# Counting more of a graph's edges: 308 nodes instead of 200, int16 counts, one-hots by ScalarE

## The chip, the cores and the metric

The kernel runs on one core of a Trainium2 chip. Its engines work side by side, each through its own queue in order: TensorE (PE; its weight loads are shown as PEld), VectorE (DVE), ScalarE (ACT), GpSimd (POOL), and SyncE (SP), which here only starts transfers. Tiles lie in SBUF, 128 partitions wide; results of matmuls lie in PSUM, which has banks of 512 f32 per partition. The metric is the time of one execution on the device, in microseconds (us). The kernel before took 1614.48 us, the median of three runs (1614.27 to 1616.7).

## The reference

One layer on 6250 nodes of 256 features and 100,000 edges, all in f32. Cut to what matters:

```
xn = layernorm(x)
neigh = segment_sum(xn[src], dst)              # one row of 256 per edge, added to its target
g = batchnorm(relu(((1 + eps) * xn + neigh) @ W1 + b1) @ W2 + b2) * gamma + beta
m = mixer(xn)                                  # linear attention over all nodes, then gelu(. @ w1) @ w2
x = x + g + m
x = x + ffn(layernorm(x))                      # an LSTM along the nodes, hidden size 256, and a gate
```

The edges come sorted by target (`dst`), and the targets are denser at the low end: a target is 6250 times the square of an even draw. So the first edges share few targets, each of which receives many rows.

## The kernel before

**Preparation (0 to about 70 us).** The rows are loaded and normalised (`xn`), written back to memory as `xn_d`, and also kept transposed (`xnT`). The sources (`si`) and targets of the edges are brought into columns: 782 edge tiles of 128 edges, in `GROUPS` = 196 groups of four (`GT` = 4). Two checks on the targets are kept in `within` (lines 289 to 309): each group's targets must span fewer than `W` = 96 nodes, and in the counted part each pair of tiles must span fewer than `CW` = 8 nodes, all below `CN`. If a check fails, a slow fallback redoes the sums (lines 740 to 775).

**The edge loop (about 72 to 909 us).** It builds `sums`, the transposed neighbour sums, in two ways.

- *The gathered part*: groups 34 to 195. For each tile GpSimd gathers 128 rows of `xn_d` (L390) into one of ten buffers `eg`. VectorE builds a selection matrix `here` from the targets (L401). TensorE multiplies them (L411), and VectorE adds the result into a window of `sums` (L421), whose place is read from a register.
- *The counted part*: the first `COUNTED` = 34 groups, 136 tiles in 68 pairs. Nothing is gathered. `count_job` makes, for each edge, a one-hot of 128 for the low bits of its source (ScalarE: `Square` of a ramp less the value, then `Relu` of 1 less that, L621 and L622) and a one-hot of 392 for the source's block of 128 and the target within the window of eight nodes (VectorE `is_equal`, L623). Their product (L629, bf16) counts how often each source occurs for each target; VectorE adds it into a window of `counts` (L636), which holds for 49 blocks of 128 sources (`NB`) `CN` = 200 targets, f32. At the end `rows_job` loads the rows of `xn_d` three blocks at a time (L646), TensorE multiplies them with the counts (L654) into one PSUM bank for both halves of the features, and VectorE adds the result to `sums` (L659).

**Other jobs in the loop.** Around the groups the kernel runs jobs written as generators. `kv_job` (50) makes keys and values and their normalisation: a matmul (L441), a bias add on VectorE (L446), a `Square` on ScalarE (L449), a reduction (L454) and a `Sqrt` on ScalarE (L456), a chain of small VectorE operations from the reciprocal (L460) to L471, then the outer products (L475, L479). `gin_job` (50) applies W1 and W2 to 125 nodes whose sums are complete (L597, L603, L608, L613). `fold_job`, `own_job` and `mix_job` belong to the mixer.

**What sets the order.** Lines 688 to 703 give every job its first slot; a slot is one turn of the loop at line 709, with one group. In every slot each running job makes one step. The order on TensorE, VectorE and ScalarE is exactly the order of issue. In a slot that order is: the gathers of the group two ahead, the add of the last group, the selections of the next, the jobs' steps by age, then the four tiles' matmuls with the jobs' matmuls spread between them, and last the variance steps of kv jobs. Transfers of `rows_job` and `own_job` stand in SyncE's queue in the same order.

**After the loop (909 us to the end).** Statistics of the batch norm, then the LSTM stage, then the output. It starts once the last gin jobs are done.

## Time and profile before

| | |
|---|---|
| median of three runs | 1614.48 us (1614.27 to 1616.7) |
| profiled execution | 1617.26 us |
| its span in the profile | 1615.2 us |
| granted TensorE clock, mean | 0.966 |
| busy: TensorE, VectorE, ScalarE, GpSimd | 1483.9, 943.9, 612.0, 680.7 us |
| gathers | 646, from 71.8 to 887.9 us, 961 ns each |
| last gin matmuls done | about 909 us |

The profile is of one execution. Busy time is the union of an engine's instructions; matmuls overlap one another, so TensorE can be shown as busy and still take more. An idle time is put down to what ended it. In the row of digits below, each digit is the busy share, in tenths, of a slice of about 40 us.

### The profile page before, as it was taken

To read this page: it belongs to the slowest core of one execution; us is meant where nothing else is said; L and a number is where in the kernel's file an instruction comes from. 1 tells how busy PE (TensorE), PEld (TensorE's weight loads), DVE (VectorE), ACT (ScalarE), POOL (GpSimd) and SP (SyncE) were. 2 spreads that over 40 slices of the span, in tenths; PEclk is the share of its full clock that TensorE was granted. 3 is DMA by queue.
4 is the path that set the end of the run, shared out by engine and by line. 5 is a ranking of instruction groups with operands and counts; after the bars stand their busy time and mean duration, and the time that the engine had idled before them with its cause. 6 is when DMAs were issued, how large, how long until landed. Compare 5 with 4: busy or idle time off the path is not lost. (4 is left out here: it accounts for less than half of the span.)

```text
span 1615.2 us, 31225 instructions
## 1 busy us (share of the span) xinstructions
PE 1483.9 (92%) x11312; PEld 1388.5 (86%) x11312; DVE 943.9 (58%) x3027; ACT 612.0 (38%) x1867; POOL 680.7 (42%) x714
## 2 busy tenths in 40 slices
PE   1789898999989999999999599999999999999984
PEld 1488788989888999999989599999999998888864
DVE  6789888888742222222222385555555557777777
ACT  2833333343312222233222255445554434444440
POOL 2177777777777777777777000000000000000005
PEclk9799999999999999999999799999999999999996
DMA  9533333333444554444444021111111002233315
GB/s 245 194 105 105 105 104 104 105 102 106 133 137 141 151 156 144 122 119 123 120 123 142 29 90 64 65 65 52 65 65 65 14 1 77 90 92 92 94 45 160
DMA packets 64645, 166.03 MB, mean 103 GB/s; under 512 B 14347, under 2 KB 29436, under 8 KB 63228
## 3 DMA queue, kind: packets, MB, share of 16 engines
q0 software_dynamic: 31008, 84.71, 18.4%
q1 hardware_dynamic: 29822, 75.08, 14.3%
q10 hardware_dynamic: 3648, 4.10, 1.1%
q8 instruction: 93, 1.52, 0.4%
q14 instruction: 74, 0.61, 0.1%
HBM read 130.56 MB, written 33.28 MB: 101 GB/s over the span
## 5 line engine op out<-in xcount | busy, mean ns | idle before, releaser
L390 POOL DMA_INDIRECT eg<-xn_d,si x646 | 620.5, 961 | 257.8 <-issue 99.3
L411 PE MATMUL pg<-here,eg 128*128 128x96 f32 x2584 | 389.1, 276 | 32.5 <-DMA eg<-xn_d,si 30.3
L411 PEld LDWEIGHTS pg<-here,eg 128*128 128x128 f32 x2584 | 358.2, 195 | 63.2 <-DMA eg<-xn_d,si 34.4
L962 ACT ACTIVATE gate<-pg,b_l 128x125 f32<-128x125 f32 x718 | 201.9, 366 | 230.4 <-PE pg L953 229.1
L421 DVE TENSOR_TENSOR sums<-sums,pg 128x192 f32 x162 | 57.3, 353 | 349.3 <-PE pg L411 202.9
L920 PE MATMUL pg<-yT,w_ih 128*128 128x125 f32 x1600 | 188.4, 276 | 0.0
L920 PEld LDWEIGHTS pg<-yT,w_ih 128*128 128x128 f32 x1600 | 184.1, 193 | 0.0
L953 PE MATMUL pg<-sums,w_hh 128*128 128x125 f32 x1568 | 183.1, 275 | 0.0
L953 PEld LDWEIGHTS pg<-sums,w_hh 128*128 128x128 f32 x1568 | 179.0, 192 | 0.0
L889 POOL TENSOR_TENSOR ln_r<-ln_v,minus_half 125x1 f32<-125x1 f32 x50 | 27.4, 552 | 350.9 <-DVE ln_v L887 314.0
L1091 POOL TENSOR_TENSOR xr<-xr,rest_t 125x1024 f32<-125x1024 f32 x8 | 22.9, 2899 | 312.3 <-DVEq L1036 312.3
L953 PE MATMUL pg<-h_w,w_hh 128*128 128x125 f32 x1248 | 145.6, 275 | 0.0
L613 ACT ACTIVATE sums<-mm,vec 128x125 f32<-128x125 f32 x100 | 36.4, 365 | 281.4 <-DVE sums L421 232.8
L953 PEld LDWEIGHTS pg<-h_w,w_hh 128*128 128x128 f32 x1248 | 143.0, 192 | 0.0
L597 PE MATMUL mm<-sums,g 128*128 128x125 f32 x800 | 116.8, 282 | 2.6 <-DVE counts L636 2.5
L608 PE MATMUL mm<-z,g 128*128 128x125 f32 x800 | 115.5, 284 | 0.8 <-DVE stats L614 0.6
L597 PEld LDWEIGHTS mm<-sums,g 128*128 128x128 f32 x800 | 103.8, 195 | 6.0 <-issue 2.3
L441 PE MATMUL mm<-m,xr 128*125 128x256 f32 x400 | 107.8, 395 | 0.6 <-DVE counts L636 0.6
L608 PEld LDWEIGHTS mm<-z,g 128*128 128x128 f32 x800 | 102.6, 197 | 1.2 <-DVE stats L614 0.8
L449 ACT ACTIVATE mm<-kv 125x512 f32<-125x512 f32 x50 | 30.1, 602 | 186.4 <-DVE kv L446 186.4
L968 DVE TENSOR_TENSOR new<-gate,gate 128x125 f32<-128x125 f32 x178 | 51.5, 289 | 65.2 <-ACT gate L962 60.3
L401 DVE TENSOR_TENSOR here<-counts,drel 128x384 f32<-128x384 f32 x162 | 89.4, 552 | 0.0
(238 smaller groups left out, 2164.6 us busy)
## 6 DMA issues: line engine op xcount, KB each, us to landing
x_d<-x_out SPq DMA_DIRECT2D x40, 500.0 KB
x_in<-x_d SPq DMA_DIRECT2D x40, 500.0 KB
eg<-xn_d,si POOLq DMA_INDIRECT x646
counts<-xn_d SPq DMA_DIRECT2D x16, 384.0 KB
xn<-in_x_dram SPq DMA_DIRECT2D x5, 1120.0 KB
xn_d<-xn SPq DMA_DIRECT2D x5, 1120.0 KB
m<-in_x_dram SPq DMA_DIRECT2D x50, 112.0 KB
out_dram<-o SPq DMA_DIRECT2D x12, 448.0 KB
```

Source lines behind the costliest of these rows:

```text
L390: nc.gpsimd.indirect_dma_start(out=g, out_offset=None, in_=xn_d[:], in_offset=bass.IndirectOffsetOnAxis(ap=at, axis=0))
L401: nc.vector.tensor_tensor(here[:, :n, :], iota[:, None, :W].to_broadcast([P, n, W]), drel[:, gi * GT:gi * GT + n, None].to_broadcast([P, n ...
L411: nc.tensor.matmul(pg[:, k, :], g[:, k * P:(k + 1) * P], here[:, i, :], start=(i == 0 and k == 0), stop=(i == n - 1), skip_group_check=True)
L421: nc.vector.tensor_add(window, window, pg)
L441: nc.tensor.matmul(pkv[:r, at], xnT[:, j, k, :], w_qkv[:, k, D:][:, at], start=(k == 0 and half == 0), stop=(k == KD - 1), skip_group_chec ...
L597: nc.tensor.matmul(p1[:, m, :], g1[:, k, m * P:(m + 1) * P], sums[:, k, at], start=(m == 0 and k == 0), stop=(k == KD - 1), skip_group_che ...
L608: nc.tensor.matmul(p2[:, a, :], g2[:, m, a * P:(a + 1) * P], z1[:, m, :], start=(a == 0 and m == 0), stop=(m == 2 * KD - 1), skip_group_ch ...
L613: nc.scalar.activation(sums[:, a, at], p2[:, a, :], AF.Identity, bias=col("gb2", a))
L920: nc.tensor.matmul(pg[:, SLOT[g], :], w_ih[:, k, block(g, a)], yT[:, k, s * NC:(s + 1) * NC], start=(i == 0 and k == 0), stop=False, skip_ ...
L953: nc.tensor.matmul(banks[a][:, SLOT[g], :], w_hh[:, k, block(g, a)], h[:, k, :], start=False, stop=(k == KD - 1), skip_group_check=True)
L962: nc.scalar.activation(gate[g], pg[:, SLOT[g], :], AF.Tanh if g == G else AF.Sigmoid, bias=bias(g, a))
L968: nc.vector.tensor_mul(new, gate[I], gate[G])
```

## The change

- The counted part grows from 34 to 42 groups (68 to 84 pairs of tiles), and from 200 to 308 nodes. The gathered loop has 154 groups instead of 162.
- `counts` are held as int16, two to a word, so that 49 blocks of 316 fit in less room than 49 of 208 f32 took. Before use, ScalarE copies three blocks at a time to f32 (a new step in `rows_job`).
- The one-hot of 392 is made by ScalarE too, with the `Square` and `Relu` of the other: per pair four Squares (of 128 and 392 columns) and one Relu of 1040 columns. The `is_equal` on VectorE goes, and with it the ramp in PSUM (`iota_p`) and ScalarE's copy into it; `zero`, eight columns in PSUM, takes its place where an addend was needed. The sign of `c_key` is turned for the bias.
- Every second pair's counts go to a PSUM bank of their own (`ps_c`) instead of the four shared ones.
- The products with the rows go to two PSUM banks, one for each half of the features; the second is the one in which the kv jobs accumulate. The final add is two instructions.
- The start slots move: counting ends at slot 88 instead of 74, loads come every 3 slots from 90 (before every 2.5 from 74), the gin jobs of the first nodes wait for slot 145 (before 119), own and mix jobs start every 1.4 slots instead of 1.5. The fold stays at slot 74.

```diff
-COUNTED = 34
-CT, CW, CN = 2, 8, 200
+COUNTED = 42
+CT, CW, CN = 2, 8, 308
...
-        counts = part(NB * (CN + CW)).rearrange("p (b n) -> p b n", b=NB)
+        counts_f = part(NB * (CN + CW) // 2)
+        counts = counts_f.bitcast(I16).rearrange("p (b n) -> p b n", b=NB)
...
+        counts_at = behind[:, 3 * RB * D:][:, :2 * RB * CN].rearrange("p (i b n) -> p i b n", i=2, b=RB)
+        HOT = P + NB * CW
+        hot = part(CT * HOT).bitcast(BF16).rearrange("p (i t m) -> p i t m", i=2, t=CT)
+        squares = part(CT * HOT)
...
-            nc.gpsimd.memset(counts, 0.0)
+            nc.gpsimd.memset(counts_f, 0.0)
...
-        iota_p = ps_c.tile([P, NB * CW], F32, name="iota_p", tag="c")
+        zero = ps_c.tile([P, 8], F32, name="zero", tag="c")
+        nc.vector.memset(zero, 0.0)
...
-        nc.scalar.copy(iota_p, iota_c)
...
-        nc.vector.scalar_tensor_tensor(c_key, bits, float(CW), c_key, op0=ALU.mult, op1=ALU.add)
+        nc.vector.scalar_tensor_tensor(c_key, bits, -float(CW), c_key, op0=ALU.mult, op1=ALU.subtract)
...
-            for i in range(CT):
-                nc.scalar.activation(squares[:, i, :], iota_c[:, :P], AF.Square, bias=c_lo[:, q * CT + i:q * CT + i + 1])
-            nc.scalar.activation(lo, squares, AF.Relu, bias=1.0, scale=-1.0)
-            nc.vector.tensor_tensor(key, iota_p[:, None, :].to_broadcast([P, CT, NB * CW]),
-                                    c_key[:, tiles, None].to_broadcast([P, CT, NB * CW]), op=ALU.is_equal)
-            yield [], None
-            pc = ps.tile([P, NB, CW], F32, name="mm")
+            for i in range(CT):
+                for minus, at in ((c_lo, slice(0, P)), (c_key, slice(P, HOT))):
+                    nc.scalar.activation(squares[:, i, at], iota_c[:, :at.stop - at.start], AF.Square,
+                                         bias=minus[:, q * CT + i:q * CT + i + 1])
+            of = hot[:, q % 2]
+            nc.scalar.activation(of, squares, AF.Relu, bias=1.0, scale=-1.0)
+            yield [], None
+            pc = ps_c.tile([P, NB, CW], F32, name="pc", tag="c") if q % 2 else ps.tile([P, NB, CW], F32, name="mm")
...
+            counts_b = counts_at[:, i % 2]
+            nc.scalar.copy(counts_b[:, :len(blocks)], counts[:, blocks[0]:blocks[-1] + 1, :CN])
             yield [], None
             if i == 0:
-                sums_c.append(ps_c.tile([P, KD, CN], F32, name="sums_c", tag="c"))
+                sums_c.append(ps_c.tile([P, BANK], F32, name="sums_c0", tag="c"))
+                sums_c.append(ps_kv.tile([P, BANK], F32, name="sums_c1", tag="acc"))
...
-                nc.tensor.matmul(sums_c[0][:, k, :], rows_b[:n, j, k * P:(k + 1) * P], counts[:n, b, :CN],
-                                 start=(b == 0 and k == 0), stop=(b == NB - 1), skip_group_check=True)
+                nc.tensor.matmul(sums_c[k][:, :CN], rows_b[:n, j, k * P:(k + 1) * P], counts_b[:n, j, :], start=(b == 0),
+                                 stop=(b == NB - 1))
...
-        COUNT_END, FOLD = 74, 74
+        COUNT_END, FOLD = 88, 74
...
-            start(COUNT_END + 2.5 * i, rows_job(i))
-        SUMMED = int(COUNT_END + 2.5 * LOADS) + 3
+            start(COUNT_END + 2 + 3 * i, rows_job(i))
+        SUMMED = int(COUNT_END + 2 + 3 * LOADS) + 4
...
-            start(FOLD + 8 + 1.5 * j, own_job(j))
-            start(FOLD + 9 + 1.5 * j, mix_job(j))
+            start(FOLD + 8 + 1.4 * j, own_job(j))
+            start(FOLD + 9 + 1.4 * j, mix_job(j))
```

## The prediction

> **What bounds the kernel now.** I read the page's first two parts, then the groups by shape, then stretches of the timeline. The page's slices show a long plateau from about 70 to 890 us: the edge loop, with GpSimd level at 7 tenths and TensorE near full.
>
> ```profile
> PE   1789898999989999999999599999999999999984
> DVE  6789888888742222222222385555555557777777
> ACT  2833333343312222233222255445554434444440
> POOL 2177777777777777777777000000000000000005
> ```
>
> A level row means pacing. The timeline of GpSimd at 600 us shows the beat: 0.95 us of gather and 0.30 us of issue, 1.25 us a tile, 5.00 us a slot of four.
>
> ```profile
> 601.01 0.95 POOL L390 DMA_INDIRECT eg<-xn_d,si  x1 [0.30 <-issue]
> 602.26 0.95 POOL L390 DMA_INDIRECT eg<-xn_d,si  x1 [0.30 <-PE pg L411]
> ```
>
> The same 0.30 us is booked to varying releasers, so it is issue cost, not waiting. The first gather starts at 71.8 and the last at 887.86: 162 slots, 5.07 us each with the odd longer beat. GpSimd sets the loop, but TensorE is close behind. Its busy digits overstate it (matmuls overlap), so I take its cost from start to start: in the trace, neighbouring f32 passes (two to a matmul) start 112 ns apart with 96 or 125 columns, 169 with 200, 216 with 256, 419 with 500; the bf16 count matmul takes 166. The timeline of TensorE agrees:
>
> ```profile
> 600.87 0.87 PE L654 MATMUL sums_c<-counts 128*128 128x200 f32 x4
> 601.57 0.58 PE L411 MATMUL pg<-here,eg 128*128 128x96 f32 x4
> ```
>
> Four passes of 200 columns occupy 0.70 us, not 0.87. Per job this gives: edge group 16 x 0.112 = 1.79 us; gin job 32 x 0.112 = 3.58; mix job 8 x 0.112 + 4 x 0.216 = 1.76; kv job 8 x 0.216 + 8 x 0.112 = 2.62; count pair 0.33; a load of three count blocks 12 x 0.169 = 2.03. As a test, slots 108 to 120 hold 58.5 us of such work and TensorE took 58.3 (625.6 to 683.9): where it is full, this sum is its time. The end of the loop also waits:
>
> ```profile
> 887.86 0.95 POOL L390 DMA_INDIRECT eg<-xn_d,si  x1 [0.30 <-PE mm L608]
> ...
> 888.10 1.08 PE L597 MATMUL mm<-sums,g 128*128 128x125 f32 x8
> ...
> 892.57 1.17 PE L411 MATMUL pg<-here,eg 128*128 128x96 f32 x4 [3.39 <-DMA eg<-xn_d,si]
> ```
>
> TensorE waits 3.39 us for the last tiles and then runs at a granted clock of 0.74 from 890 to 910 (windows view).
>
> **The Trainium skill.** "TensorE: Matmul & The Clock Gate", Part 1 (HAM clock gate), says that an idle window of about 3.4 us halves the clock; the 3.39 us wait followed by 0.74 agrees. "ScalarE: Activation LUTs", What ACT_TABLE_LOAD costs, prices an ACTIVATE at 186 ns + 0.833 ns a column, 93 more with a pointer bias, and 93 of overlap between neighbours. The trace agrees: 128 columns with a bias 388 ns (the price says 386), 256 without 417 (399).
>
> ```profile
> L623 DVE TENSOR_TENSOR counts<-iota_p,counts 128x784 bf16<-128x784 f32 x68 | 65.5, 963 | 0.0
> ...
> L621 ACT ACTIVATE counts<-counts 128x128 f32<-128x128 f32 x136 | 46.2, 388 | 0.0
> ...
> L636 DVE TENSOR_TENSOR counts<-counts,mm 128x392 f32 x68 | 37.8, 556 | 1.9 <-PE mm L441 0.9 <-issue 0.7 <-PE pg L411 0.4
> ```
>
> "VectorE: DVE Perf Modes", Why PSUM operands drop a tier, leaves no fast mode to an f32 PSUM operand, so the int16 count add, still reading PSUM, should keep its 556 ns; no run here shows int16.
>
> **The change part by part.**
>
> *Eight groups leave the edge loop* (162 slots to 154): GpSimd loses 32 gathers, 8 x 5.07 = 40.6 us; TensorE loses 8 x 1.79 = 14.3.
>
> *Sixteen more count pairs* add 16 x 0.33 = 5.3 us of TensorE. *308 columns in place of 200* in 196 passes: from the slope between 256 and 500 columns (0.832 ns) a pass takes 259 ns, 90 more, 17.6 us. TensorE's net is +8.6 us, in a loop whose feed became 40 us shorter. The gain can't be 40.
>
> *Where TensorE becomes the bound.* The loads now run from slot 92 to 140 beside mix jobs (every 1.4 slots) and gin jobs whose rate rises towards the end. From slot 90 on the changed loop holds 64 groups 113.8 us, 65 half gin jobs 116.5, 45 mix firsts and 46 seconds 80.1, 196 passes x 0.259 = 50.8: 361 us, 5.6 a slot against the 5.07 that GpSimd needs. So GpSimd waits for buffers there and TensorE sets the time. Before, the stretch from slot 90 (533.1) to the last gin matmul (909.0) took 375.9 with 351 of work. To 361 I add stalls: the gin products read `sums` after the group add on VectorE, which in turn waits for TensorE's earlier slot; a few tenths for each of 32 gin jobs, and a tail of dependent gin jobs. I take 7 us (0 to 12). The late landing and the half clock of the old end go, since the gathers then run ten tiles ahead. Stretch: 368 against 375.9, -7.9 us (-15 to -3).
>
> *One-hots by ScalarE, slots 0 to 89.* VectorE loses 0.96 us a pair (L623). ScalarE's pair grows from 1.13 us (two Squares, a Relu) to four Squares (386, 605, 386, 605 less three overlaps: 1.70) and a Relu of 1040 columns (1.05 to 1.07): 2.78 us, 84 times, in a 5.07 us slot. Average load is fine; the order is what matters. In a slot ScalarE does the kv Square, then the one-hots, then the kv Sqrt, for which VectorE's next kv chain stands waiting with everything queued behind it: the group add, selections, count add, next kv add.
>
> ```profile
> 332.95 0.68 DVE L446 TENSOR_TENSOR kv<-mm,m 125x512 f32<-125x512 f32 x1
> ...
> 333.67 0.60 ACT L449 ACTIVATE mm<-kv 125x512 f32<-125x512 f32 x1 [4.36 <-DVE kv L446]
> ...
> 334.20 0.68 ACT L621 ACTIVATE counts<-counts 128x128 f32<-128x128 f32 x2
> ...
> 335.35 0.21 ACT L456 ACTIVATE kv_s<-kv_v 125x16 f32<-125x16 f32 x1
> ```
>
> This is the round in the timeline. After: chain 1.77 (329.10 to 330.87), kv add 0.72, Square 0.53, one-hots 2.78, Sqrt 0.26: 6.1 us between consecutive kv jobs. Of seven slots five start a kv job; across a free slot the round also holds a group add, selections and two count adds' pitches, about 7.2 for two slots. Seven slots: 3 x 6.1 + 2 x 7.2 = 32.7, 4.7 a slot, inside 5.07. But twelve gin jobs start in slots 20 to 70, each with some 2.2 us on ScalarE (four Relus 1.2, two sums with a VectorE step between, 1.0): +0.5, so 5.2 there. 50 slots x 0.13 = 6.5 us late. The ten tile buffers (12.5 us, of which landing needs 3) absorb about 6, and slots 72 to 90 hold only 71 us of TensorE work in 91 us to catch up; but time that GpSimd has stood still isn't caught up. I charge +2.5 us, between 0 and 10: a round 5% longer costs another ten less the cushion.
>
> *At nothing or nearly so.* The count adds (as above; at twice the price 84 x 0.56 us in VectorE's freed time). Copying counts to f32: 17 x 0.96 us by the same ScalarE price, a slot ahead of use; uncovered they would cost 16. The second PSUM bank: one bank's 512 f32 can't hold 616, and the kv accumulator's is free after the fold; odd pairs in their own bank relieve the shared four. Memset smaller, under the first loads. The 17 loads on SP's queue move to slots 90 to 138, two slots before use, ahead of own-row loads queued behind them; if a load were late its products stall TensorE and the own loads, but it has 10 us for 384 KB. The last weights for the next stage are issued nearer to its start, yet some 20 us before first use. Without the ScalarE copy of `iota_p` (0.49 us) the start gains about 0.5, hidden under gathers unless TensorE is late; I drop it.
>
> Sum: +2.5 - 7.9 = -5.4. The profiled execution took 1617.26 (span 1615.2 and 2.06 around it), 2.8 above the median; taking the difference off the median 1614.48 gives **1609**.
>
> **Rivals.**
> 1. *GpSimd stays the bound* (for: no gather shows a real wait now; against: 5.6 us a slot of TensorE work from slot 90). It would give -40, with the tail more: 1574. Chance 0.03.
> 2. *The ScalarE round takes over* (slower): VectorE waits for Sqrt behind the one-hots. Each 0.1 us on the round is 0.1 x 70 = 7 us less cushion; from about 0.15 us beyond my 6.1 it passes the 7.9 gained. At 6.35 the early stretch costs 12 to 14: 1619. For: VectorE is queued behind it in order, and any half-clock spell after TensorE's waits adds. Against: VectorE is 0.96 us lighter. Chance 0.24.
> 3. *It comes out even*, stalls of 12 in the late stretch and +2.5 before: 1614. Chance 0.15.
> 4. *The counted path does not apply*: each pair's 256 edges must span under 8 nodes and stay under 308, else the slow fallback runs. In the reference's inputs the widest of the 84 pairs spans 7 and the highest node is 283. Chance 0.01; milliseconds.
>
> My forecast (1601 to 1612) has 0.57.
>
> **How the numbers follow.** Measurement of this kernel tells about 0.2%, 3.2 us. Ends: -15 with nothing early gives 1600; -3 with +10 gives 1622. 1600 to 1622 holds the forecast, the even case and most of rival 2; outside are rival 1, the fallback, and a worse round. Faster 0.60 (forecast and rival 1), same 0.15, slower 0.25.
>
> **What would show it.** Right: gathers with waits well over 0.30 us from about slot 95, TensorE without gaps to the end, L654's pass near 259 ns, no DMA wait of 3 us at the last group, the loop's end near 903. The ScalarE group for 1040 columns near 1.07 us and gathers held up little before slot 70. Wrong: gathers stalled between slots 20 and 72 by over 5 us, with VectorE idle before the kv reciprocal, or TensorE gaps before count matmuls; or late-stretch time beyond 373.

## The result, and the profile after

The changed kernel takes 1626.1 us (median of seven runs, 1622.31 to 1633.62). The kernel before, run beside it, takes 1616.52 (1614.27 to 1619.06). The ratio is 1.0061, with a 95% interval of 1.0039 to 1.0083: the change makes the kernel slower, by little. Measured once more, beside e10 and e11 below (e12), it was 1.0034 (1.0022 to 1.0047). The forecast was 1609, with a range to 1622.

The profiled execution took 1623.33 us, its span is 1621.5, which is 6.3 more than the 1615.2 of before. I split this at the first matmul of slot 90, as the prediction did:

| us | before | after | difference | forecast |
|---|---|---|---|---|
| slot 72 begins on TensorE | 441.1 | 459.2 | +18.1 | |
| slot 90 begins on TensorE | 533.1 | 543.5 | +10.4 | +2.5 (0 to 10) |
| from there to the last gin matmul | 375.9 | 371.8 | -4.1 | -7.9 (-15 to -3) |
| TensorE at half clock, slots 3 to 90 | 10.2 | 45.3 | | |

So the loss arises early, before slot 72. 7.7 us of it are made up by slot 90, where the prediction had counted 71 us of TensorE work in 91 us. The gain of the late stretch comes, but half as large. Against the forecast of -5.4, the profile is 11.7 us off: 7.9 of it ahead of slot 90, 3.8 behind.

The page's busy digits of after, 40 slices of about 40 us each, and the granted clock below them:

```profile
PE   2799999899999999999999799999999999999984
DVE  6777666667663222222222385555555556777776
ACT  2866666666785323323333254455544434444440
POOL 1177777667777777766675000000000000000005
PEclk9699989999999999999999899999999999999996
```

VectorE has gone from 8 to 6 or 7 tenths up to slice 10, and ScalarE from 3 to 6 or 7, as the change intends. No engine is full by these digits. But GpSimd shows 6 in the eighth and ninth slices (284 to 365 us), where it had an even 7: gathers have been held up. The groups by shape (busy us, mean ns) show that the prices were right:

```profile
L621 ACT ACTIVATE counts<-counts 128x392 f32<-128x392 f32 x168 | 102.3, 609 | 0.0
L624 ACT ACTIVATE counts<-counts 128x1040 bf16<-128x1040 f32 x84 | 89.9, 1070 | 2.7
L621 ACT ACTIVATE counts<-counts 128x128 f32<-128x128 f32 x168 | 65.7, 391 | 0.2
L657 PE MATMUL sums_c<-counts 128*128 128x308 f32 x192 | 56.2, 427 | 0.0
L636 DVE TENSOR_TENSOR counts<-counts,pc 128x392 f32 x42 | 25.1, 597 | 2.9 <-issue 1.3 <-PE mm L442 0.6 <-PE pg L412 0.5
```

The four Squares and the Relu of a pair take 1.70 + 1.07 = 2.77 us in the timeline, as forecast (2.78). The estimates that the prediction worked out from "ScalarE: Activation LUTs", What ACT_TABLE_LOAD costs, were 605 ns for 392 columns and 1052 for 1040: 4 and 18 ns under the measurement. The int16 count add takes 597 ns instead of 556. The passes over 308 columns start 261 ns apart in the trace (forecast 259).

What moved is who waits. The waits between 90 and 455 us (the stretch with one-hots), some lines of the view, first before, then after; the columns are the total wait, how often, and the longest:

```profile
POOL eg L390 <- PE pg L411: 25.9, 85, 0.3
DVE sums L421 <- PE mm L597: 8.4, 7, 2.4
PEld L629 <- ACT counts L622: 4.9, 6, 0.9
PE mm L629 <- ACT counts L622: 2.9, 4, 0.8
DVE kv_v L454 <- ACT mm L449: 1.3, 2, 0.7
```

```profile
POOL eg L391 <- PE pg L412: 35.8, 81, 2.9
DVE kv_v L455 <- ACT mm L450: 32.7, 49, 0.7
DVE sums L422 <- PE mm L598: 15.4, 6, 3.9
PE pc L629 <- ACT counts L624: 12.2, 9, 2.4
DVE kv_r L461 <- ACT kv_s L457: 7.6, 28, 0.3
PE mm L629 <- ACT counts L624: 7.4, 9, 2.1
```

Before, the gathers' longest wait put down to TensorE was the 0.30 us of issue. Now it is 2.9 us. TensorE's matmuls waited 2.9 us in all for ScalarE's one-hots; now 12.2 + 7.4 = 19.6, up to 2.4 at a time. VectorE now waits for ScalarE at the `Square` of every kv job (49 times) and at the `Sqrt` of over half of them (28 times). And where a gin job's first products run (L598), its group add waits for TensorE up to 3.9 us at a time.

The timeline of one round shows the order that makes it so (kv job to kv job, both with one-hots between):

```profile
292.41 0.25 DVE L461 RECIPROCAL kv_r<-kv_s 125x16 f32<-125x16 f32 x1
...
294.16 0.68 DVE L447 TENSOR_TENSOR kv<-mm,m 125x512 f32<-125x512 f32 x1
294.88 0.60 ACT L450 ACTIVATE mm<-kv 125x512 f32<-125x512 f32 x1 [2.50 <-DVE kv L447]
295.42 1.70 ACT L621 ACTIVATE counts<-counts 128x128 f32<-128x128 f32 x4
297.15 1.07 ACT L624 ACTIVATE counts<-counts 128x1040 bf16<-128x1040 f32 x1
298.13 0.20 ACT L457 ACTIVATE kv_s<-kv_v 125x16 f32<-125x16 f32 x1
298.28 0.83 PE L629 MATMUL pc<-counts 128*128 128x392 bf16 x2 [2.38 <-ACT counts L624]
298.36 0.25 DVE L461 RECIPROCAL kv_r<-kv_s 125x16 f32<-125x16 f32 x1 [0.24 <-ACT kv_s L457]
```

ScalarE idles 2.50 us for VectorE's chain and add, then does the one-hots, and VectorE can't begin the next chain until the `Sqrt` behind them. No engine is busy all the time, yet the round is closed: 292.41 to 298.36, 5.95 us. The forecast had 6.1. Before, a single round took 5.71 us (median): VectorE alone filled it, with some 0.3 us of idle time. TensorE stands 2.38 us before the count product, with the group's and the gin job's matmuls queued behind. A few microseconds later GpSimd, with its ten buffers in use, stands too:

```profile
299.35 0.94 POOL L391 DMA_INDIRECT eg<-xn_d,si  x1 [0.30 <-issue]
301.46 0.94 POOL L391 DMA_INDIRECT eg<-xn_d,si  x1 [1.17 <-PE pg L412]
304.02 0.95 POOL L391 DMA_INDIRECT eg<-xn_d,si  x1 [1.62 <-PE pg L412]
306.62 0.95 POOL L391 DMA_INDIRECT eg<-xn_d,si  x1 [1.65 <-PE pg L412]
```

The last three of these ought each to start 1.25 us after the one ahead of it. The forty gathers from slot 40 to 49 take 9.0 us more than 1.25 each (before: 1.4).

A measure that can be read from every trace is the pace of the kv jobs. Their reciprocals (L460 before, L461 after) mark the rounds. From kv job 15 to job 45 there are 42 slots: 216.0 us before (5.14 a slot) and 230.8 after (5.50; 5.41 in e12). The forecast charged 5.2.

### The profile page after: what moved, and what is told of

It is laid out like the page before. It is cut to its first block, busy times and chain, and to the rows that moved or that the text cites. A ratio compares the mean times of both kernels' runs of the same rounds, so it can differ in the third digit from the quotient of the medians.

```text
span 1621.5 us, 31140 instructions
## 1 busy us (share of the span) xinstructions
PE 1493.5 (92%) x11216; PEld 1389.1 (86%) x11216; DVE 897.5 (55%) x2961; ACT 778.5 (48%) x2099; POOL 649.0 (40%) x682
## 5 line engine op out<-in xcount | busy, mean ns | idle before, releaser
L391 POOL DMA_INDIRECT eg<-xn_d,si x614 | 590.9, 962 | 295.0 <-PE pg L412 105.1
L412 PE MATMUL pg<-here,eg 128*128 128x96 f32 x2456 | 371.7, 277 | 15.8 <-DMA eg<-xn_d,si 14.5
L412 PEld LDWEIGHTS pg<-here,eg 128*128 128x128 f32 x2456 | 346.4, 197 | 38.5 <-DMA eg<-xn_d,si 13.8
L621 ACT ACTIVATE counts<-counts 128x128 f32<-128x128 f32 x336 | 143.5, 500 | 0.2
L614 ACT ACTIVATE sums<-mm,vec 128x125 f32<-128x125 f32 x100 | 36.3, 364 | 218.1 <-DVE sums L422 196.5
L598 PE MATMUL mm<-sums,g 128*128 128x125 f32 x800 | 117.6, 285 | 0.0
L598 PEld LDWEIGHTS mm<-sums,g 128*128 128x128 f32 x800 | 106.5, 199 | 1.9 <-issue 0.4
L624 ACT ACTIVATE counts<-counts 128x1040 bf16<-128x1040 f32 x84 | 89.9, 1070 | 2.7
```

The costliest lines, as they stand in the source:

```text
L391: nc.gpsimd.indirect_dma_start(out=g, out_offset=None, in_=xn_d[:], in_offset=bass.IndirectOffsetOnAxis(ap=at, axis=0))
L412: nc.tensor.matmul(pg[:, k, :], g[:, k * P:(k + 1) * P], here[:, i, :], start=(i == 0 and k == 0), stop=(i == n - 1), skip_group_check=True)
L598: nc.tensor.matmul(p1[:, m, :], g1[:, k, m * P:(m + 1) * P], sums[:, k, at], start=(m == 0 and k == 0), stop=(k == KD - 1), skip_group_che ...
L621: nc.scalar.activation(squares[:, i, at], iota_c[:, :at.stop - at.start], AF.Square, bias=minus[:, q * CT + i:q * CT + i + 1])
L624: nc.scalar.activation(of, squares, AF.Relu, bias=1.0, scale=-1.0)
```

## The experiments

Theory, after the result: ScalarE and VectorE form a closed round because the one-hots stand ahead of the `Sqrt` in ScalarE's queue. It fills the slots from about 20 to 72 and holds up everything behind. Rivals: the larger sizes are the cause, in either stretch; TensorE's cooled clock is the cause; TensorE's load is the cause.

Seven of the kernels were measured where the kernel before itself took 1761 to 1780 us instead of 1617; they are told of together at the end. Each trace is of one execution.

**The key's one-hot on VectorE again, the rest of the change kept (e1).**

```diff
-                for minus, at in ((c_lo, slice(0, P)), (c_key, slice(P, HOT))):
...
+                nc.scalar.activation(squares[:, i, :P], iota_c[:, :P], AF.Square, bias=c_lo[:, q * CT + i:q * CT + i + 1])
...
-            nc.scalar.activation(of, squares, AF.Relu, bias=1.0, scale=-1.0)
+            nc.scalar.activation(of[:, :, :P], squares[:, :, :P], AF.Relu, bias=1.0, scale=-1.0)
+            nc.vector.tensor_tensor(of[:, :, P:], iota_p[:, None, :].to_broadcast([P, CT, NB * CW]),
+                                    c_key[:, q * CT:(q + 1) * CT, None].to_broadcast([P, CT, NB * CW]), op=ALU.is_equal)
...
-            pc = ps_c.tile([P, NB, CW], F32, name="pc", tag="c") if q % 2 else ps.tile([P, NB, CW], F32, name="mm")
+            pc = ps.tile([P, NB, CW], F32, name="mm")
```

The ramp in PSUM comes back with it and takes the bank of its own that every second pair's counts had.

> The changed kernel with the one-hot of the key made by VectorE again (is_equal from the ramp in PSUM), all growth kept: 42 groups, 308 nodes, int16 counts, two banks. Theory (the longer one-hots on ScalarE make TensorE wait and cool in slots 0 to 89, +10.4 us in the profile): the first group matmul of slot 90 comes near 533 us as in the kernel before instead of 543.5, the stretch from there to the last gin matmul stays near 372, so about 1613 us, some 10 to 13 below the changed kernel and 3 to 4 below the kernel before. Rival (int16 counts, the copies or the later slots cost it): slot 90 stays near 543 and the time near 1626.

Measured: 1613.84 us against 1617.31 before, ratio 0.9975 (0.9966 to 0.9985). Pace 5.15 us a slot, slot 90 at 532.0, the late stretch 371.9. Its waits from 90 to 455 us:

```profile
ACT mm L450 <- DVE kv L447: 181.7, 49, 5.9
...
POOL eg L391 <- PE pg L412: 32.3, 106, 0.3
```

The gathers' longest wait is 0.3 us again, and TensorE's matmuls wait 2.0 us in all for ScalarE's one-hots, 2.9 before. So the early loss belongs to this edit, and the larger sizes, the int16 counts, the copies and the two banks of the products together cost nothing early. (The bank of every second pair went with the edit; e3 below keeps it and is as fast.) The growth alone gains 0.25%, about 4 us, nearly all of it late.

**The change's machinery at the old sizes (e2).**

```diff
-COUNTED = 42
-CT, CW, CN = 2, 8, 308
+COUNTED = 34
+CT, CW, CN = 2, 8, 200
```

and the start slots of before. The int16 counts, the copies and all the banks stay as in the changed kernel.

> The changed kernel with the sizes and slots of before (34 groups, 200 nodes, counting to slot 74, loads every 2.5 slots, mix every 1.5), but with one-hots by ScalarE, int16 counts, copies and two banks. Theory: the early stretch loses what it loses in the changed kernel, slot 90 near 541 to 544 instead of 533, and as GpSimd sets the later stretch nothing is won back: about 1624 us, 8 to 10 over the kernel before. Rival (the growth costs it): as the kernel before, 1616.

Measured: 1626.11 us, ratio 1.0059 (1.004 to 1.0078); pace 5.39, slot 90 at 541.6. At old sizes too, the one-hots on ScalarE cost about 9.5 us (0.59% of 1617). With e1 this makes a square of four kernels: the step to ScalarE costs 9.5 us at the old size and 9.5 to 14 at the new one (ratio 0.9975 without it, 1.0034 and 1.0061 with it), the growth gains 4 us or less.

**The one-hots behind the kv `Sqrt` (e3).** The same work on the same engine, in another place: issued with the last steps of a slot, into three buffers, and multiplied a slot later.

```diff
-            for i in range(CT):
-                for minus, at in ((c_lo, slice(0, P)), (c_key, slice(P, HOT))):
...
-            of = hot[:, q % 2]
...
+            of = hot[:, q % 3]
...
+            def one_hots():
+                for i in range(CT):
+                    for minus, at in ((c_lo, slice(0, P)), (c_key, slice(P, HOT))):
...
+                nc.scalar.activation(of, squares, AF.Relu, bias=1.0, scale=-1.0)
...
+            yield [], one_hots
             yield [], None
```

> The changed kernel with the one-hots issued at the end of a slot, behind the Sqrt of the kv job, into three buffers, and their product a slot later. The same work on every engine. Theory (it is the place of the one-hots in the round VectorE chain, kv add, Square, one-hots, Sqrt that costs, not their amount): the round shrinks from 6 us to 3.3, TensorE finds the one-hots ready, the waits for L624 and most half-clock spells before slot 90 go, slot 90 near 533 to 535, about 1613 to 1616 us. Rival (ScalarE simply has too much to do): slot 90 near 543, about 1626.

Measured: 1613.36 us (1609.34 to 1620.88, 17 runs), ratio 0.9977 (0.9965 to 0.999). This is e1's time with none of the work taken off ScalarE. So the load as such costs hardly anything; what costs is where and when the one-hots are made. The run does not part two things: they no longer stand ahead of the `Sqrt`, and their product comes a slot later, with a third buffer, so that TensorE has no reason to wait for them. A kernel with the later product alone was not measured. One thing more is not clean. The profiled execution was the slowest of the 17. In it the waits for one-hots are gone from TensorE, but the pace is 5.34, slot 90 comes at 537.4, and 44 us are at half clock between slots 3 and 90. Its waits:

```profile
ACT mm L450 <- DVE kv L447: 58.7, 39, 3.3
ACT kv_s L457 <- DVE kv_v L456: 49.5, 49, 1.2
...
POOL eg L391 <- PE pg L412: 34.0, 93, 1.4
```

ScalarE now waits for VectorE ahead of the `Sqrt`, not VectorE for ScalarE's one-hots; the single rounds are 5.6 us (median). Two free-slot rounds of 11.85 and 11.49 us hold 6.5 us of what this execution takes longer than e1's between jobs 15 and 45 (8.0 in all), and 9.8 us at half clock lie in them; the explanation below comes back to such rounds. What set off the half clock here is open.

**Products of 200 columns (e4)**, to see whether TensorE's work limits the late stretch. The counts of targets 200 to 307 are left out of the sums.

```diff
-                nc.tensor.matmul(sums_c[k][:, :CN], rows_b[:n, j, k * P:(k + 1) * P], counts_b[:n, j, :], start=(b == 0),
+                nc.tensor.matmul(sums_c[k][:, :200], rows_b[:n, j, k * P:(k + 1) * P], counts_b[:n, j, :200], start=(b == 0),
```

> The changed kernel with 200 columns in the count products and in the final add; the counts of targets 200 to 307 are left out of the sums. Theory (from slot 90 TensorE sets the time): its work there falls by 196 x 0.09 = 17.6 us, and the stretch from slot 90 by 12 to 17 us, down to where GpSimd sets it; about 1611 to 1614 us. Rival (that stretch is held by waits between VectorE, ScalarE and TensorE or by the gathers): under 5 us less, above 1621.

Measured: 1607.12 us, ratio 0.9942 (0.9922 to 0.9963). The late stretch takes 356.2 us, 15.6 less than after, for 17.6 us less work (196 passes by 90 ns). From slot 90 on TensorE's work sets the time, nearly one for one, as forecast; the time itself came out 4 us below the forecast's 1611. Slot 90 comes at 542.2, about as in the changed kernel (543.5, and 541.6 in e12).

**A filler on TensorE (e7).** One f32 matmul of 392 columns ahead of each pair's products: TensorE works where it had waited.

```diff
             def count(i):
+                if i == 0:
+                    nc.tensor.matmul(pc.rearrange("p b n -> p (b n)"), ident, iota_c, start=True, stop=True)
```

> The changed kernel with one more matmul ahead of each pair's count products (an f32 identity on the ramp, 392 columns, into the pair's own bank, overwritten by the products that follow): 2 passes of 0.33 us, 84 times, 55 us more for TensorE in slots 1 to 85, done while TensorE would wait for the one-hots. Theory with cooling as its larger part (a wait of 2.4 us by itself would be caught up; the half-clock spells that follow it are what fills the buffers): the half-clock spells between 90 and 480 us shrink from 41 us in the profile to under 20, and slot 90 comes no later than 543.5 us, perhaps 538; time 1620 to 1626. Rival (the waits alone cost it, the clock hardly matters): added work only delays, slot 90 near 550 or later, 1632 or more.

Measured: 1631.43 us (1629.92 to 1632.88), ratio 1.0089 (1.0076 to 1.0102). Between slots 3 and 90 only 0.1 us were at half clock, so this did what it should. Slot 90 came at 549.6, 6.1 later than in the changed kernel, though the filler is some 55 us of work. The time as a whole is near the rival's. Yet the rounds show both sides. The four free-slot rounds that were longest in the changed kernel (46.98 us together) take 40.15, and the eight others between jobs 15 and 45 take 8.5 us more. So the full clock did give time back, and the filler's own work spent it elsewhere. The filler as a remedy gains nothing.

**A small filler (e11)**, of 96 columns, about 19 us in all.

```diff
+                if i == 0:
+                    nc.tensor.matmul(pc.rearrange("p b n -> p (b n)")[:, :96], ident, iota_c[:, :96], start=True, stop=True)
```

> The light filler again, for the same reason. Where the kernel before takes about 1617 us: theory (cooling adds to the waits) half-clock spells of slots 3 to 90 below 20 us and slot 90 before 541, 1 to 5 us below the changed kernel beside it; rival (the round sets the early stretch) slot 90 between 542 and 548 with the spells gone, the time not below the changed kernel's.

Measured: 1628.17 us, ratio 1.005 (1.0034 to 1.0065), beside the changed kernel's 1.0034 (1.0022 to 1.0047). The time at half clock between slots 3 and 90 was 33.4 us, and 31.2 in the changed kernel beside it. So it did not keep TensorE warm, and says nothing for or against the cooling; it gains nothing. Slot 90 came at 547.1.

**One more Square in each pair (e10).** ScalarE's round becomes 0.29 us longer, 24.6 us over 84 pairs, and TensorE's and VectorE's work stays.

```diff
-                for minus, at in ((c_lo, slice(0, P)), (c_key, slice(P, HOT))):
+                for minus, at in ((c_lo, slice(0, P)), (c_key, slice(P, HOT)), (c_lo, slice(0, P)))[:3 - i]:
```

> The kernel with one Square made twice, again, since the chip of its first run fed the gathers at 6 us a slot instead of 5.07. Where the kernel before takes about 1617 us: theory (the round fills the slots) 1638 to 1645, slot 90 at 556 to 562; rival (ScalarE has room) under 1632, slot 90 before 549.

**The changed kernel beside it (e12).**

> The changed kernel itself, beside the two: 1622 to 1630 where the kernel before takes about 1617; if this chip too feeds the gathers at 6 us a slot, some 1725 to 1735 against 1760, since GpSimd's 32 gathers fewer are then worth 48 us and the longer slots cover the one-hots.

Measured: e10 takes 1642.66 us, ratio 1.0137 (1.0116 to 1.0158); e12 1623.85, ratio 1.0034 (1.0022 to 1.0047). Of the 24.6 us added, 18.8 show in the time. Slot 90 comes at 562.4, in e12 at 541.6. The single rounds (median) grow from 5.94 to 6.27, the pace from 5.41 to 5.71: the 0.29 us arrives in full. TensorE's waits for the one-hots grow with it, and so does its time at half clock between slots 3 and 90 (61.4 us, in e12 31.2), so the 18.8 need not be the longer round alone. From the chain of waits, 90 to 455 us, e12 first:

```profile
PE pc L629 <- ACT counts L624: 12.8, 8, 2.4
PE mm L629 <- ACT counts L624: 7.7, 10, 2.5
```

```profile
PE pc L629 <- ACT counts L624: 22.9, 11, 2.8
PE mm L629 <- ACT counts L624: 13.9, 11, 2.7
```

An engine at 6 to 7 tenths busy passes on three quarters of what is added to it. That is what being on a closed round means.

**Half of the products in the early gin jobs left out (e16).** By the prediction's own prices TensorE has 34 us of work in seven slots here (7 x 1.79 of groups, 5 x 2.62 of kv, 7 x 0.33 of pairs, and 12 gin jobs in 50 slots, 6.0), of 35.5. So I had come to think that TensorE can't make up its waits.

```diff
-        def gin_job(b):
+        def gin_job(b, parts=KD):
...
-            yield [partial(first, m, k) for m in range(2 * KD) for k in range(KD)], None
+            yield [partial(first, m, k) for m in range(2 * KD) for k in range(parts)], None
...
+            start(at, gin_job(b, 1 if at < 70 else KD))
```

> The changed kernel with half of the products left out in the gin jobs before slot 70 (21.5 us of TensorE work fewer, wrong results for these nodes), again, as the last chip was one that feeds gathers at some 6 us a slot. On one that feeds them at 5.07 us: theory (TensorE is full in the early stretch and can't make up its waits) pace of kv jobs 15 to 45 5.10 to 5.25 us a slot, slot 72 at 443 to 451, time 1611 to 1619; rival (the round of ScalarE and VectorE alone) pace 5.35 to 5.50, slot 72 at 454 to 460, time 1621 to 1628.

Measured: 1623.74 us (12 runs), ratio 1.0014 (0.9996 to 1.0033). The profiled execution (1624.62) has the rival's numbers: pace 5.40, slot 72 at 459.4. TensorE's waits for one-hots grew by nearly the time that its work shrank (21.5 us):

```profile
PEld L629 <- ACT counts L624: 41.1, 27, 2.5
...
PE pc L629 <- ACT counts L624: 20.3, 15, 2.5
PE mm L629 <- ACT counts L624: 17.6, 12, 2.5
```

20.3 + 17.6 = 37.9 us, against 19.6. In this execution less work on TensorE did not change the pace. But the half clock went up to 54.6 us between slots 3 and 90 (30.7 between jobs 15 and 45, in e12 13.6), so the run took work away and added cooling, and does not show that either is free. And five of the twelve times lie at 1614.6 to 1619.2, seven at 1623.7 to 1627.7, while the changed kernel's fifteen (e12 among them) all lie at 1622.3 or above. The traced one is of the upper group; there is no trace of the lower one. So TensorE's load seems to have a part in the early loss in some executions; what tells these from the others stays open.

**Own and mix jobs earlier (e6; e1 with one edit).** Now the other direction. Since slots 72 to 90 have room and the late stretch is TensorE's, work should move forward.

```diff
-            start(FOLD + 8 + 1.4 * j, own_job(j))
-            start(FOLD + 9 + 1.4 * j, mix_job(j))
+            start(FOLD + 7 + 1.25 * j, own_job(j))
+            start(FOLD + 8 + 1.25 * j, mix_job(j))
```

> The changed kernel with the key's one-hot on VectorE, and own and mix jobs one slot earlier and every 1.25 slots instead of 1.4, so that they end at slot 143 instead of 151. Theory (TensorE sets the time from slot 90, but not between 72 and 90): only what moves ahead of slot 90 is gained, 2 to 3 mix jobs of 1.76 us, and the end loses work that had no cover: 3 to 6 us under the one without the move (1613.8), 1608 to 1611. Rival (order in the late stretch doesn't matter): 1613 to 1614.

Measured: 1610.17 us, ratio 0.9952 (0.994 to 0.9965). Slot 90 at 534.3, 2.3 later than in e1, and the late stretch 368.0, 3.9 shorter.

**And the loads earlier (e5; e6 with the last pairs two to a slot).**

```diff
-            start(q * (COUNT_END - 3) / PAIRS, count_job(q))
+            start(min(q, 70 + (q - 70) / 2), count_job(q))
...
-            start(COUNT_END + 2 + 3 * i, rows_job(i))
+            start(80 + 3.6 * i, rows_job(i))
```

and four buffers of one-hots instead of two.

> As the one before, and the last 14 pairs are counted two to a slot, so that counting ends at slot 77 and the loads begin at slot 80, every 3.6 slots (four buffers for one-hots). Theory: three loads of 3.1 us go ahead of slot 90 into slots where TensorE had 20 us to spare: 8 to 10 us less again, 1599 to 1603. Rival (the gain is eaten by VectorE or ScalarE in slots 70 to 78, or by the loads' transfers beside the own rows): 1608 or more.

Measured: 1599.93 us (1599.13 to 1601.5), ratio 0.9891 (0.9877 to 0.9906). This beats both kernels, by 1.1% and by some 1.6%. Slot 90 comes at 538.3, 6.2 after e1's, and the stretch from there takes 354.6 instead of 371.9. The changed kernel was not measured beside it, so the 1.6% compares two medians.

**Seven kernels where gathers were fed more slowly (e8, e9, e13, e14, e15, e17, e18).** e8 and e9 are the edits of e10 and e11, e13 that of e16, e14 and e17 the kernel e3. e15 and e18 leave one Square out:

```diff
-                for minus, at in ((c_lo, slice(0, P)), (c_key, slice(P, HOT))):
+                for minus, at in ((c_lo, slice(0, P)), (c_key, slice(P, HOT)))[i if q > 0 else 0:]:
```

> The changed kernel with one Square of 128 columns made twice in every pair: 0.29 us more of ScalarE, 84 times, 24.6 us in all; nothing else differs. Theory (the one-hots lie in a round through VectorE and ScalarE that already fills the slots from 20 to 70, with the tile buffers used up): nearly all of it from slot 20 on shows, slot 90 moves from 543.5 to 556 to 562 us, the time to 1638 to 1645. Rival (ScalarE has room, 778 us busy of 1621, and single waits and cold spells cost it): slot 90 moves by under 5 us, the time stays under 1632.

> The changed kernel with a filler matmul ahead of each pair's products as in the filler run, but with 96 columns: 2 passes of 0.112 us, 19 us of work in place of 55. Theory (cooling adds to the waits): if it too keeps the half-clock spells of slots 3 to 90 below 20 us (45 in the changed kernel), slot 90 comes before 541 us and the time is 1 to 5 us below the changed kernel's 1626. Rival (the round sets the early stretch, and a warm clock gains nothing): slot 90 stays between 542 and 548 with the spells gone, the time at 1626 or above.

> The changed kernel with half of the products left out in the gin jobs that start before slot 70 (12 jobs, 16 passes of 112 ns each fewer: 21.5 us of TensorE work; every step of ScalarE and VectorE stays; their results are wrong for these nodes). In the profiles of the changed kernel the kv jobs 15 to 45 (42 slots) go at 5.50 and 5.41 us a slot, against 5.14 before. Theory (TensorE has about 34 us of work in seven slots of 35.5 there, so its waits for the one-hots can't be made up): the pace falls to 5.10 to 5.25, slot 72 comes at 443 to 451 rather than 457 to 459, time 1611 to 1619. Rival (the round of ScalarE and VectorE alone sets the pace, TensorE has room): the pace stays at 5.35 to 5.50, slot 72 at 454 to 460, time 1621 to 1628.

> The kernel with the one-hots behind the kv Sqrt once more, since the profiled execution was the slowest of its 17. Theory (the place in the queue is what cost): in an ordinary execution no TensorE wait for one-hots, pace of kv jobs 15 to 45 at 5.12 to 5.25 us a slot (5.34 in the slow one), slot 90 at 532 to 536, time 1610 to 1616. Rival (the load of ScalarE is what costs, wherever it stands): pace 5.3 to 5.5, slot 90 at 538 to 544, time 1620 to 1626.

> The changed kernel with one Square of 128 columns fewer in each pair from the second on (left out: the low one-hot of every second tile keeps an old value, the counts are wrong): ScalarE's round is 0.29 us shorter, 24 us in all, TensorE's work is unchanged. If ScalarE's round is on the path from both sides (one more Square cost 18.8 us), the single rounds fall from 5.95 to 5.66, the pace of kv jobs 15 to 45 to 5.15 to 5.25 us a slot and the time to 1612 to 1617, no lower, since GpSimd's 5.07 us takes over. If the round is only a cost above a threshold that the changed kernel just reaches, the same gain shows with the waits for one-hots below half of their 44 us. Rival (TensorE alone sets the pace): less than 3 us gained, 1621 to 1626.

> The kernel with the one-hots behind the kv Sqrt again, for a trace of an ordinary execution at gathers of 5.07 us a slot. If the place in ScalarE's queue is what cost: no TensorE wait for one-hots, pace of kv jobs 15 to 45 at 5.12 to 5.25 us a slot (5.41 to 5.50 in the changed kernel, 5.14 before), slot 90 at 532 to 536, time 1610 to 1616. If ScalarE's load costs wherever it stands: pace 5.3 to 5.5, slot 90 at 538 to 544, time 1620 to 1626.

> The changed kernel with one Square of 128 columns fewer in each pair from the second on (left out: the low one-hot of every second tile keeps an old value, the counts are wrong), again, at gathers of 5.07 us a slot. After the half-products run the round of ScalarE and VectorE is the theory: single rounds of kv jobs at 5.66 instead of 5.95, pace of jobs 15 to 45 down by 0.2 to 0.3 us to 5.12 to 5.25, time 1612 to 1617. If something else sets the pace: less than 3 us gained, 1621 to 1626.

| kernel | us | before beside it | ratio (95%) |
|---|---|---|---|
| e8, one more Square | 1731.77 | 1762.59 | 0.9835 (0.9814 to 0.9856) |
| e9, small filler | 1728.62 | 1762.59 | 0.9805 (0.9786 to 0.9823) |
| e13, half products | 1741.42 | 1780.2 | 0.9779 (0.9755 to 0.9803) |
| e14, behind the `Sqrt` | 1738.67 | 1780.2 | 0.977 (0.9745 to 0.9795) |
| e15, one Square fewer | 1739.66 | 1780.2 | 0.979 (0.976 to 0.9819) |
| e17, behind the `Sqrt` | 1726.05 | 1761.01 | 0.979 (0.9757 to 0.9823) |
| e18, one Square fewer | 1728.7 | 1761.01 | 0.9794 (0.9757 to 0.9831) |

None of their questions is answered. The pace of kv jobs 15 to 45 is 5.98 to 6.14 us a slot in all seven alike, whatever their round. The gathers' durations are unchanged (958 ns in e17), but more of the starts come late. Waits of e17 (GpSimd, 90 to 800 us):

```profile
POOL eg L391 <- issue: 104.8, 334, 1.4
POOL eg L391 <- PE pg L412: 95.3, 93, 2.0
POOL eg L391 <- remote: 26.8, 22, 2.1
```

What does show is that the sign of such a change depends on how fast the gathers are fed. At 6 us a slot, eight groups fewer are worth about 48 us by estimate, and all these kernels beat the one before by 1.7 to 2.3%. It is no property of one chip: e5, e6 and e7 ran on the same chip as e13 to e15, at another time, with the kernel before at 1617. The cause is open. Whether a round shorter than the changed kernel's gives time back at the usual pace wasn't measured either, since both kernels with one Square fewer fell here.

## Why the prediction was wrong

*What bounds the kernel: right.* GpSimd paces the loop and TensorE is close behind; e4 shows TensorE's work as the bound after slot 90.

*"One-hots by ScalarE, slots 0 to 89": this step failed.* It charged +2.5 us (0 to 10), and the profile shows +10.4 (8.5 in e12). VectorE does wait for the `Sqrt` behind the one-hots, the operation prices were right, and so was the single round (6.1 forecast, 5.95 measured in 26 of 30, within 0.1). But this wait is the small part. e1 has the same start slots, so it can be set against the changed kernel round by round. Between jobs 15 and 45 the changed kernel takes 14.5 us longer than e1 (10.8 in e12):

| rounds, jobs 15 to 45 | after less e1, us | e12 less e1, us |
|---|---|---|
| 14 single ones without a gin job's last step | +2.8 | +2.8 |
| 4 single ones with it | +3.6 | +3.6 |
| 4 across a free slot (jobs 17, 22, 29, 32) | +12.7 | +9.0 |
| the other 8 across a free slot | -4.6 | -4.6 |

Two terms of the sum were mis-sized:

- *The gin jobs: "+0.5" by averages, so 5.2 a slot.* The last step of a gin job runs by turns, ScalarE, VectorE, ScalarE, VectorE (L614, L615), ahead of the count add and the next chain. I had priced it as ScalarE time (1.0) and spread it over seven slots. In the changed kernel it stands behind the one-hots on ScalarE, so VectorE waits 1.5 us for it instead of 0.4. The round from 310.49 to 318.49 shows it:

```profile
315.26 1.07 ACT L624 ACTIVATE counts<-counts 128x1040 bf16<-128x1040 f32 x1
...
316.34 0.35 ACT L614 ACTIVATE sums<-mm,vec 128x125 f32<-128x125 f32 x1
316.72 0.30 DVE L615 BATCH_NORM_STATS2 stats<-mm 128x6 f32<-128x125 f32 x1 [1.04 <-ACT sums L614]
317.05 0.37 ACT L614 ACTIVATE sums<-mm,vec 128x125 f32<-128x125 f32 x1 [0.36 <-DVE stats L615]
317.45 0.30 DVE L615 BATCH_NORM_STATS2 stats<-mm 128x6 f32<-128x125 f32 x1 [0.43 <-ACT sums L614]
```

The four single rounds that hold it take 7.94 to 8.00 us, in e1 6.99 to 7.12; without it a single round takes 5.94. In a closed round the whole length of such a step is added where it falls.

- *The round across a free slot: 7.2 us, with TensorE left out of it.* The one round in which VectorE had neither a gin job's last step nor a wait for TensorE took 7.33 us (from 264.26), so 7.2 was right for two engines. Over all 19 the mean is 9.4. The longest are the four of the table: 12.10, 11.73, 12.13 and 11.02 us, in e1 8.35 to 9.12. In these VectorE's group adds wait 4.0 to 5.0 us for TensorE. TensorE had stood 1.1 to 2.4 us for the one-hots, had a gin job's first products still to do, and was at half clock for 3.4 to 6.2 us of each round. The sum has no term for this; rival 2 has it ("any half-clock spell after TensorE's waits adds").

*How much of that is the clock?* One round tells. In both traces of the changed kernel TensorE waits 2.38 us for the one-hots just ahead of job 29's round and then does the same 70 matmuls in it. In the trace of after a spell at half clock begins during the wait, in e12 none does. After, then e12 (the stretch, its length, busy time of TensorE, of its weight loads, of VectorE, ScalarE and GpSimd, the granted clock, the DMA's share and GB/s):

```profile
298.36:310.49 12.13, 12.13 (x70) 11.51 (x70) 5.88 (x17) 7.23 (x16) 6.48 (x8) 0.77 0.26 76
```

```profile
298.31:307.69 9.38, 9.38 (x70) 8.86 (x70) 5.86 (x17) 7.24 (x16) 6.81 (x8) 1.00 0.34 99
```

TensorE is busy from end to end, and 12.13 x 0.77 = 9.3: the difference is the clock. The four rounds together hold 20.1 us at half clock in after and 12.5 in e12; at half a microsecond lost for each, the estimate is 10 us of the 12.7 and 6 of the 9.0. The whole difference between these two executions over the 42 slots (3.7 us) lies in these four rounds. In e7, without half clock and with 5.3 us of filler in them, they take 40.15 us together, near e1's 34.3 plus the filler. So the cooled clock, which the waits for one-hots bring, is the largest single part of the early loss between jobs 15 and 45 in these traces. What half clock costs in other rounds is not worked out here.

For seven slots, the unit of the sum, these 42 slots make 38.5 us; the sum had 32.7, and 36.4 with the gin jobs. They take 14.8 us longer than before (230.8 less 216.0), most of the +18.1 at slot 72. The buffers' cushion of "about 6" was there: the gathers were 4.5 us ahead of their use at slot 20 and 11.1 at slot 40 (before 4.1 and 7.8). Then it was used up, and GpSimd stood still. The slack of slots 72 to 90 gave 7.7 back, which the prediction had named and not counted, "time that GpSimd has stood still isn't caught up". That part was wrong in the other direction: the tiles lay ready in the buffers, and TensorE caught up.

*"Where TensorE becomes the bound": right, its size off.* Forecast 361 of work and 7 of stalls (0 to 12), measured 371.8, so 10.8 of stalls, inside the range. The waits of after from 543.5 to 915.3 us name over half:

```profile
POOL eg L391 <- PE pg L412: 59.6, 101, 3.5
...
PE mm L563 <- DVE stats L615: 5.9, 7, 1.9
```

The mix job's first matmuls wait 5.9 us for VectorE's statistics of a gin job. The rest stays open. The gathers wait up to 3.5 us for buffers, so GpSimd is no longer the bound there, as forecast. From 870 to 910 us the granted clock is 1.00 (0.87 before): the late landing and the half clock of the old end are gone, as said.

*At nothing: right as a sum.* e1 holds these edits but the bank of every second pair, and loses nothing early (slot 90 at 532.0 against 533.1). The count add did become 41 ns dearer; "VectorE: DVE Perf Modes", Why PSUM operands drop a tier, had led me to expect no change.

*Rival 1* (GpSimd stays the bound, 1574) is out at the usual pace of gathers. *Rival 2* is what happened, at 1626 instead of 1619, but not by its arithmetic: that needed a single round of 6.25 us or more, and the single round came out below the forecast. What made it true is its clause on TensorE's waits and the half clock. *Rival 3*'s stalls of 12 in the late stretch came true (10.8), but not its +2.5.

## What to carry to other kernels

When work moves to an engine with room, don't compare its average load with the slot: lay out one round of the in-order queues, with each operation at the place where it stands, and do so for the rounds that hold other jobs as well, for there each extra operation counts in one piece. Follow the delay on to TensorE: a wait of 2.4 us there can bring a spell at half clock, and in a round that TensorE fills the spell cost more than the wait. Work that nobody waits for at once belongs behind the operation that closes a round, with its product late enough that it finds it ready (e3 did both at once). And when a change makes an engine the bound in one stage, look for the stage beside it that has slack and move work there (e5), before expecting the gain.

## What was unexpected of the hardware

- Short waits were enough for half clock. In the trace of after TensorE waited 2.38 us for the one-hots from 242.1, 295.9 and 322.0 us; spells of 3.4 to 6.8 us began at 242.6, 297.2 and 324.5, inside the wait or at its end. "TensorE: Matmul & The Clock Gate", Part 1 (HAM clock gate), speaks of an idle window of about 3.4 us. Here, ahead of the eight spells from 89.0 to 512.3 us, TensorE is shown idle for only 0.8 to 2.4 of the 3.4 us before each. And the same wait need not have the same end: after 2.38 us from 295.8 in e12 no spell came.
- The early stretch has more than one outcome with the same program: the twelve times of e16 fall into two groups, 1614.6 to 1619.2 and 1623.7 to 1627.7. What picks the group is open; between the two traced executions of the changed kernel, four rounds with more or less half clock made 3.7 us.
- The feed of the gathers allowed 5.07 us a slot in most measurements (the kernel before) and some 6.0 in the seven kernels above, on one chip in both ways, with unchanged durations of the single gather (962 ns in the changed kernel, 958 in e17).
